# Thought's weights prepared inside the first attention, its first chain ahead of the next scans' preparation, and its gate behind the rounds

## The chip, the cores and the metric

The kernel runs on one core of one Trainium2 chip. The metric is the device time of one execution, in microseconds, the median of three runs. Five engines share the core: TensorE (PE in the profile; its weight loads are a row of their own, PEld), VectorE (DVE), ScalarE (ACT), GpSimd (POOL) and SyncE (SP), which issues the DMAs. Each engine works through its own instructions in program order and waits on semaphores for the others.

## The reference

The whole is a small decoder of four layers with four batches of 256 tokens, 256 channels, all in float32. Each part is added to x and followed by a plain layer norm. The parts that matter here, cut down:

```python
# part 0: attention of 16 heads of 128, one shared key and value head, rotary, causal
x = layernorm(x + attn0(x))
# part 1: a selective scan over another input, ctx, gated by x
def ssm(ctx, x):
    u = silu(conv4(ctx @ in_proj.T) + conv_b)           # 256 channels, 256 steps
    dt, Bm, Cm = split(u @ x_proj.T, [8, 16, 16])
    delta = softplus(dt @ dt_proj.T + dt_b)
    state = exp(delta * A) * state + delta * u * Bm      # 16 states per channel
    y = sum_n(state * Cm) + D * u
    return y * silu(x)
x = layernorm(x + ssm(ctx, x))
# part 2: the "thought": one vector per batch, from the last token
t = (ln(x[:, -1]) * in_g + in_b) @ agg_w + agg_b
for _ in range(4):
    h = gelu((ln(t) * pn_g + pn_b) @ d1_w + d1_b)        # 256 -> 1024
    t = t + h @ d2_w + d2_b                              # 1024 -> 256
out = x + sigmoid(x @ gate_w + gate_b) * (t @ bc_w + bc_b)
x = layernorm(x + ln(out) * out_g + out_b)
# part 3: attention with 16 heads of 16, 4 key and value heads
x = layernorm(x + attn3(x))
# part 4: a second selective scan over ctx with other weights, gated by x
x = layernorm(x + ssm(ctx, x))
# parts 5 to 11: experts, a state space layer, cross attention, a ternary
# feed-forward, linear attention, attention to ctx, a float8 feed-forward
```

The scans of parts 1 and 4 depend on ctx alone until their last product with silu(x). They can therefore run long before x is known, and the kernel uses that.

## The kernel before, in words

x stays in SBUF as eight tiles of 128 tokens by 256 channels, and its transpose xT beside it. The parts follow each other; when one runs, the weights of the next are loaded by a call named `more`. Work is issued from Python in one order; the order of instructions on each engine follows that, with moves that the scheduler makes from what each instruction waits for.

**First attention and first scans.** `run_mqa` has 32 steps (4 batches, 4 groups of 4 heads, 2 tiles of queries). A step n divides its softmax (`shares`), makes the scores of n+1 and the queries of n+4, puts two steps of the first scans (called l0x) beside that, then turns its probabilities on TensorE, and multiplies them with the values (`sums`); the `output` matmul follows a step later. At n = 6 it calls `more`, which loads the thought's weights. For each batch whose attention and scans are done, `gate_pair` (L534) multiplies y with silu(x), transposes it and adds it to x. This runs two steps into the next batch, and for the last batch after the loop; then L388 starts the preparation of the second scans (l1x).

**Scans.** `_steps` of class `Scans` is a generator. Its first part is the preparation: four taps by DMA and GpSimd, eight convolution matmuls of 512 columns into one PSUM bank, Silu on the whole (L126), two matmuls for dt, B and C (L474 and a DMA to DRAM), and softplus as Abs, Exp, Ln on du of 128x2048 and a `scalar_tensor_tensor` on VectorE (L120). GpSimd then makes du = delta * u (L123). After it come 64 steps (4 batches, 16 states): a DMA that spreads B and C over the partitions, two Exp for dA on ScalarE, s = du * B on VectorE (L111), the scan instruction (L520), s * C on VectorE, and a sum on TensorE one or two steps later. In all a step takes VectorE three instructions.

**Thought.** `run_thought` first prepares its weights: the columns of d2 are centred, so that the mean of t's increment is zero, by a reduction over 128x2048 on VectorE (L129) and eight Identity on ScalarE; constants `over`, `less`, `power`, `pick` and `centre` are filled by GpSimd and VectorE; d1b is joined with pn_b @ d1 by `quarters` (four quarters of the 1024 columns on four groups of 32 partitions); d1 is scaled with pn_g; cb is the centred d2b. Then it makes the gate of all eight tiles, 16 matmuls, 8 additions, one Sigmoid. After these comes the chain: the last tokens are transposed (L684), normed, multiplied with agg, centred. The four rounds follow, each: square, variance by matmul, a power on GpSimd, scaling, `quarters` with d1, Gelu, two transposes (L728), a copy (L730), `quarters` with d2, a copy (L734), sums with `pick`. GpSimd meanwhile makes gx = gate * bc_b + x and xb = x + out_b. Then 24 scan steps of l1x are issued, `K.scans.beside(24)`. The tail is per batch: `gated` multiplies the gate with t @ bc_w and adds gx on GpSimd, `moments` takes its statistics with a root on GpSimd (L169 and a power at L123), `added` norms it into x, and `settle` applies the part's layer norm (L160, L161, L117) and transposes x.

**Second attention.** `run_gqa` starts with memsets of kn, qn and vt on GpSimd (L994 to L1001), projects and norms its queries and keys, and runs with one scan step of l1x beside each of its own steps.

TensorE's accumulators live in PSUM[...]. The thought has a pool `thp` of three, `thf` of one; the scans have one.

## Time and profile before

| | us |
|---|---|
| three runs | 2458.55, 2461.45, 2464.18 |
| median | 2461.45 |
| profiled execution, its own time | 2461.66 |
| its span, first to last instruction | 2459.9 |
| TensorE busy in the span | 2267.6 (92%) |
| VectorE busy | 1464.3 (60%) |
| ScalarE busy | 801.9 (33%) |
| GpSimd busy | 288.5 (12%) |
| mean granted TensorE clock | 0.947 |

The page gives busy time for the whole span. The change touches about its first third, and there the shares are different from stage to stage, so the views that are read are the table of stretches (busy time of each engine between two times) and the instructions of one engine in order of time. In the latter, a line is start, length, engine, line of the code, operation, output<-inputs, shape, count, and in square brackets the idle time of the engine just before and the instruction that ended it. "x4" means that four like instructions are gathered in the line and the length is the sum of them. A clock of 0.50 means that TensorE was granted half of its full speed. Times are from the span's start. Marks: the first scan of l0x starts at 87.95, the first attention ends at about 366, the first scan of l1x starts at 439.23, the thought's tail begins at 499.60, the second attention's first matmul starts at 527.71.

### The profile page before, as it was taken

What the parts mean: (1) busy time and instruction counts of PE and PEld (TensorE: products, weight loads), DVE (VectorE), ACT (ScalarE), POOL (GpSimd) and SP (SyncE); (2) the same over time, 40 slices, a digit from 0 to 9 for tenths busy, and PEclk for the clock granted to TensorE, in tenths of its full rate; (3) what the DMA queues carried; (4) which work ended last, traced back from release to release, by engine and by line L of the source; (5) the groups of instructions that cost most, each with busy time, mean ns of one, the idle gap of its engine ahead of it and who ended that gap; (6) DMA issues with size and microseconds to landing.
All of it is one profiled execution on the core that took longest, in us unless ns stands there. A gap on an engine that the chain in (4) does not pass through costs nothing. (4 is left out here: it accounts for less than half of the span.)

```text
span 2459.9 us, 28697 instructions
## 1 busy us (share of the span) xinstructions
PE 2267.6 (92%) x10620; PEld 1520.1 (62%) x10624; DVE 1464.3 (60%) x2986; ACT 801.9 (33%) x1781; POOL 288.5 (12%) x455
## 2 busy tenths in 40 slices
PE   8899997769996999899999999999999988899997
PEld 4566763335433555536888888888776543476774
DVE  4799982888985211280455544445556677774566
ACT  3577664513441111162211111111022244343434
POOL 0000014130010322200011000110210002100001
PEclk9999997767887999999999999999998899999999
DMA  6222221312213544220222112110100002100000
GB/s 201 61 60 60 53 61 27 80 41 48 52 39 101 164 131 127 81 78 9 73 82 87 46 46 73 47 63 31 46 22 1 20 18 71 41 1 1 1 1 18
DMA packets 132835, 138.99 MB, mean 57 GB/s; under 512 B 13876, under 2 KB 120726, under 8 KB 130904
## 3 DMA queue, kind: packets, MB, share of 16 engines
q1 hardware_dynamic: 132696, 137.16, 19.5%
q8 instruction: 84, 1.38, 0.2%
q14 instruction: 55, 0.45, 0.1%
HBM read 134.27 MB, written 2.85 MB: 56 GB/s over the span
## 5 line engine op out<-in xcount | busy, mean ns | idle before, releaser
L132 PE MATMUL ps<-xw,xcT 128*128 128x256 f32 (+1 forms) x2304 | 518.9, 382 | 0.3 <-ACT YT L126 0.3
L132 PEld LDWEIGHTS ps<-xw,xcT 128*128 128x128 f32 x2304 | 430.8, 190 | 64.0 <-issue 1.9
L132 PE MATMUL sc<-kT,qT 32*128 32x256 f32 (+2 forms) x1024 | 239.2, 404 | 9.6 <-DVE qn L129 9.2
L132 PEld LDWEIGHTS sc<-kT,qT 128*128 128x128 f32 (+1 forms) x1024 | 152.6, 200 | 86.0 <-issue 52.4
L111 DVE TENSOR_TENSOR xp<-ps,xb 128x256 f32<-128x256 f32 x96 | 40.4, 421 | 230.7 <-PE ps L132 230.6
L126 ACT ACTIVATE dA<-delta,negA 128x255 f32<-128x255 f32 x256 | 118.2, 501 | 142.0 <-DVE s L520 139.1
L132 PE MATMUL ssmps<-s,idz 128*128 128x512 f32 x256 | 146.7, 678 | 18.9 <-DVE s L111 18.0
L520 DVE TENSOR_TENSOR_SCAN s<-dA,s 128x512 f32<-128x512 f32 x128 | 155.0, 1218 | 2.6
L126 ACT ACTIVATE p<-sc,nm 128x256 f32<-128x256 f32 (+1 forms) x256 | 112.0, 444 | 96.5 <-DVE nm L129 90.5
L111 DVE TENSOR_TENSOR hT<-u,a 128x512 f32<-128x512 f32 x48 | 33.1, 690 | 184.0 <-PE u L132 184.0
L126 ACT ACTIVATE sq<-xp 128x1024 f32<-128x1024 f32 x24 | 25.4, 1057 | 314.1 <-DVE xp L111 314.1
L132 PE MATMUL o<-pT,vt 128*128 128x256 f32 (+1 forms) x352 | 116.2, 452 | 12.3 <-ACT pT L332 11.9
L169 POOL TENSOR_SCALAR rstd<-mv 128x2 f32<-128x2 f32 x48 | 11.8, 245 | 887.5 <-DVE mv L161 877.7
L129 DVE TENSOR_REDUCE qn<-sc 128x2 f32<-128x480 f32 (+1 forms) x192 | 87.0, 505 | 37.9 <-PE sc L132 36.4
L126 ACT ACTIVATE e<-sT 128x512 f32<-128x512 f32 x128 | 70.9, 591 | 108.4 <-PE sT L132 108.2
L132 PE MATMUL sT<-q,kT 32*128 32x256 f32 (+1 forms) x384 | 102.3, 508 | 3.5 <-ACT e L126 3.3
L1474 DVE TENSOR_TENSOR_SCAN dec<-xT,idz 128x256 f32<-128x256 f32 (+1 forms) x192 | 89.7, 535 | 21.5 <-DMA xT<-ad 21.5
L129 DVE TENSOR_REDUCE nm<-sc 128x2 f32<-128x512 f32 (+1 forms) x128 | 77.3, 612 | 41.2 <-PE sc L132 40.7
L126 ACT ACTIVATE a<-g 128x512 f32<-128x512 f32 x48 | 28.7, 598 | 206.2 <-PE g L132 203.4
L111 DVE TENSOR_TENSOR s<-du,bc 128x512 f32<-128x512 f32 x128 | 87.7, 691 | 11.0 <-POOL du L123 7.7
L123 POOL TENSOR_TENSOR xp<-xp,rn 128x128 f32<-128x128 f32 x96 | 35.2, 403 | 476.9 <-DVE rn L1406 476.9
L132 PE MATMUL g<-xT,wj 128*128 128x512 f32 x192 | 90.3, 593 | 0.7 <-ACT rows L100 0.7
(503 smaller groups left out, 4027.2 us busy)
## 6 DMA issues: line engine op xcount, KB each, us to landing
bc<-bcd SPq DMA_DIRECT2D x128, 256.0 KB, 4.6
xw<-in_l2a_xw_dram SPq DMA_DIRECT2D x24, 768.0 KB, 4.8
xT<-ad SPq DMA_DIRECT2D x12, 1024.0 KB, 4.3
wj<-in_l1f_gate_dram SPq DMA_DIRECT2D x48, 128.0 KB, 2.7
wj<-in_l1f_up_dram SPq DMA_DIRECT2D x48, 128.0 KB, 2.9
wj<-in_l1f_down_dram SPq DMA_DIRECT2D x48, 128.0 KB, 3.1
sel<-cwd SPq DMA_DIRECT2D x32, 192.0 KB, 3.2
sel<-cwd SPq DMA_DIRECT2D x32, 128.0 KB, 3.5
```

Source lines behind the costliest of these rows:

```text
L111: self.nc.vector.tensor_tensor(out=out, in0=a, in1=b, op=op)
L123: self.nc.gpsimd.tensor_tensor(out=out, in0=a, in1=b, op=op)
L126: self.nc.scalar.activation(out, in_, func, **kw)
L129: self.nc.vector.tensor_reduce(out=out, in_=in_, axis=AX.X, op=op, **kw)
L132: self.nc.tensor.matmul(out, lhsT=lhsT, rhs=rhs, start=start, stop=stop)
L169: self.nc.gpsimd.tensor_scalar(out=out, in0=in_, scalar1=add, scalar2=None, op0=ADD)
L520: nc.vector.tensor_tensor_scan(out=s.rearrange("p c l -> p (c l)"), data0=dA.rearrange("p c l -> p (c l)"), data1=s.rearrange("p c l -> p ...
L1474: nc.vector.tensor_tensor_scan(out=dec[:, k, h, :], data0=ap[:, h, at(bb, k, j) : at(bb, k, 2)], data1=K.idz[:, 0 : (2 - j) * P], initial=0.0,
```

## The change

(a) The thought's weights are prepared by a generator `ready_thought`, which `run_mqa` creates at n = 6 and advances by one piece per step from n = 10 on. Two things in it are new: the sums of d2 are made on ScalarE by eight Copy instructions with an accumulated output in place of the reduction on VectorE, and its two PSUM tiles come from the shared pool of transposes. The tiles that it fills live in the weights' pool.

(b) The preparation of the l1x scans is no longer started at the end of the first attention but in `run_thought`, after the first chain (`th`, `ct` and the first part of `last`) and ahead of the rounds.

(c) In the preparation of both scans Exp and Ln are issued per half of du (128x1024), and du = delta * u is a VectorE instruction.

(d) The gate's matmuls and additions come behind the rounds, three tiles in each of the first two and two in the third, with a PSUM pool of one bank for them; the Sigmoid is issued in the third round.

(e) gx and xb are gone: bc_b is added into the PSUM tile by one more matmul with the identity, gate + x is a VectorE instruction, and out_b is added to x in place on GpSimd in the tail.

(f) Five memsets of the second attention go from GpSimd to VectorE.

```diff
--- before.py
+++ after.py
@@ -374,7 +374,9 @@
             if n in (2, 3, 4, 5):
                 rest.pop(0)()
             if n == 6:
-                more()
+                ready = ready_thought(K, more()) if K.fused(0) else iter(())
+            if n > 9:
+                next(ready, None)
             K.scans.beside(2)
             turn(n)
             if n:
@@ -385,7 +387,6 @@
         output(N - 1)
         if K.fused(0):
             gate_pair(K, wk, y, B - 1)
-            K.scans.begin("l1x")
 
 
@@ -480,11 +481,12 @@
                 K.ts(delta[:, c, s], ps, cols[:, c, 1:2], None, ADD)
                 K.act(du[:, c, s], ps, AF.Abs, bias=cols[:, c, 1:2])
-        K.act(du, du, AF.Exp, scale=-1.0)
-        K.act(du, du, AF.Ln, bias=K.eps[1.0])
+        for func, kw in ((AF.Exp, dict(scale=-1.0)), (AF.Ln, dict(bias=K.eps[1.0]))):
+            for c in range(DC):
+                K.act(du[:, c, :], du[:, c, :], func, **kw)
         for c in range(DC):
             K.stt(delta[:, c, :], delta[:, c, :], 0.0, du[:, c, :], MAX, ADD)
-            K.ptt(du[:, c, :], delta[:, c, :], u[:, c, :], MUL)
+            K.tt(du[:, c, :], delta[:, c, :], u[:, c, :], MUL)
         turn = 0
         self.y = u
@@ -557,8 +559,6 @@
             ctx.enter_context(K.turns())
             for b in range(B):
                 gate_pair(K, wk, y, b)
-        if pre == "l0x":
-            K.scans.begin("l1x")
     return run
 
@@ -579,7 +579,67 @@
     w["cols"] = K.load(wp, "l0f_cols", [P, 2, DC])
     w["pn"] = K.load(wp, "l0f_pn", [P, 2, DC])
     w["rows"] = K.load_rows(wp, "l0f_rows")
+    for n, cols in (("mean", 8), ("junk", D), ("over", P), ("less", P), ("centre", P), ("power", B), ("pick", B), ("cb", DC)):
+        w[n] = wp.tile([P, cols], F32, name=n)
     return w
+
+def quarters(K, ps, lhsT, rhs, n, start):
+    for c in range(DC):
+        for g in range(4):
+            K.mm(ps[32 * g : 32 * g + n], lhsT(c, g), rhs(c, g), start and c == 0, c == DC - 1)
+
+def quarter(d1):
+    return lambda c, g: d1[:, c, g * D : (g + 1) * D]
+
+def ready_thought(K, w):
+    nc, d1, d2, mean = K.nc, w["d1"], w["d2"], w["mean"]
+
+    for f in range(8):
+        K.act(w["junk"], d2[:, f, 0:D], AF.Copy, scale=1.0 / D, accum_out=mean[:, f : f + 1])
+        if f % 4 == 3:
+            yield
+    K.ts(d2[:, :, D], mean, 1.0, None, MUL)
+    K.ts(mean, mean, -1.0, None, MUL)
+    yield
+    for f in range(8):
+        K.act(d2[:, f, 0:D], d2[:, f, 0:D], AF.Identity, bias=mean[:, f : f + 1])
+        if f % 2:
+            yield
+    nc.gpsimd.memset(w["over"], 1.0 / D)
+    nc.gpsimd.memset(w["less"], -1.0 / D)
+    K.ts(w["centre"], K.ident, 1.0 / D, None, SUB)
+    nc.gpsimd.memset(w["power"], -0.5)
+    pick = w["pick"]
+    K.ptt(pick, K.ident[:, 0:B], K.ident[:, 32 : 32 + B], ADD)
+    for g in (2, 3):
+        K.ptt(pick, pick, K.ident[:, 32 * g : 32 * g + B], ADD)
+    yield
+    ps = K.tp.tile([P, 512], F32, name="ps", tag="tp")[:, 0:D]
+    K.mm(ps, K.ident, w["d1b"], True, False)
+    quarters(K, ps, lambda c, g: w["pn"][:, 1, c : c + 1].to_broadcast([P, B]), quarter(d1), B, False)
+    nc.scalar.copy(w["d1b"], ps)
+    yield
+    for c in range(DC):
+        K.act(d1[:, c, :], d1[:, c, :], AF.Copy, scale=w["pn"][:, 0, c : c + 1])
+        yield
+    ps = K.tp.tile([P, 512], F32, name="ps", tag="tp")
+    centred(K, w, ps[:, 0:DC].unsqueeze(2), w["cols"][:, 1, :].unsqueeze(2))
+    nc.vector.tensor_copy(w["cb"], ps[:, 0:DC])
+    yield
+
+def centred(K, w, ps, src):
+    for c in range(DC):
+        for k in range(DC):
+            K.mm(ps[:, c, :], w["centre" if c == k else "less"], src[:, k, :], c + k == 0, c + k == 2)
 
 def run_thought(K, w, more):
@@ -592,6 +652,7 @@
         wk = ctx.enter_context(tc.tile_pool(name="th2", bufs=2))
         ctx.enter_context(K.turns())
         pm = ctx.enter_context(tc.tile_pool(name="thp", bufs=3, space=PSUM))
+        gp = ctx.enter_context(tc.tile_pool(name="thg", bufs=1, space=PSUM))
         spare = ctx.enter_context(tc.tile_pool(name="thf", bufs=1, space=PSUM))
         def moments(t, rows, n):
@@ -621,63 +682,12 @@
             K.ts(r, t[:, 0, :], mv[:, 0, 0:1], rstd, SUB, MUL)
             return r
-
-        d1, d2 = w["d1"], w["d2"]
-        mean = one.tile([P, 8], F32, name="mean")
-        K.reduce(mean, d2[:, :, 0:D], ADD)
-        K.ts(d2[:, :, D], mean, 1.0 / D, None, MUL)
-        K.ts(mean, mean, -1.0 / D, None, MUL)
-        for f in range(8):
-            K.act(d2[:, f, 0:D], d2[:, f, 0:D], AF.Identity, bias=mean[:, f : f + 1])
...
+        if K.first == 2:
+            for _ in ready_thought(K, w):
+                pass
+        d1, d2, d1b = w["d1"], w["d2"], w["d1b"]
         d2b = w["cols"][:, 1, :]
-        cb = one.tile([P, DC], F32, name="cb")
-        nc.vector.tensor_copy(cb, centred(d2b.unsqueeze(2), 1)[:, :, 0])
-
-        gate = one.tile([P, NT, D], F32, name="gate")
-        for i in range(NT):
-            ps = pm.tile([P, D], F32, name="ps", tag="mm")
-            for c in range(DC):
-                K.mm(ps, K.xT[:, c, i * P : (i + 1) * P], w["gate"][:, c, :], c == 0, c == DC - 1)
-            K.tt(gate[:, i, :], ps, row["gate_b"], ADD)
-        K.act(gate, gate, AF.Sigmoid)
+        over, power, pick, cb = w["over"], w["power"], w["pick"], w["cb"]
         last = K.tp.tile([B, D], F32, name="last", tag="tp")
         for c in range(DC):
@@ -694,17 +704,17 @@
                 K.mm(ps[:, c, :], w["agg"][:, k, c * P : (c + 1) * P], xn[:, k, :], c + k == 0, c + k == 2)
         th = one.tile([P, DC, B], F32, name="th")
         K.tt(th, ps, wide(w["cols"][:, 0, :], B), ADD)
-        ct = centred(th, B)
+        ct = pm.tile([P, DC, B], F32, name="ps", tag="mm")
+        centred(K, w, ct, th)
         K.stt(th, wide(d2b, B), 4.0, th, MUL, ADD)
         last = spare.tile([P, B], F32, name="last")
         for k in range(DC):
             K.mm(last, over, th[:, k, :], k == 0, False)
-        gx = one.tile([P, NT, D], F32, name="gx")
-        xb = one.tile([P, NT, D], F32, name="xb")
-        if K.first == 2:
-            K.scans.begin("l1x")
+        K.scans.begin("l1x")
+        gate = one.tile([P, NT, D], F32, name="gate")
+        gates = iter(range(NT))
         for k in range(4):
             sq = wk.tile([P, DC, B], F32, name="sq")
             K.act(sq, ct, AF.Square)
@@ -720,7 +730,7 @@
             K.tt(cs, ct, wide(cb, B), ADD)
             ps = pm.tile([P, D], F32, name="ps", tag="mm")
             K.mm(ps, K.ident, d1b, True, False)
...
             ct = pm.tile([P, DC, B], F32, name="ps", tag="mm")
@@ -737,24 +747,29 @@
             for c in range(DC):
                 K.mm(ct[:, c, :], add[:, c * P : (c + 1) * P], pick, False, c == DC - 1)
             K.mm(last, add[:, D : D + 1].to_broadcast([P, P]), pick, False, k == 3)
+            for i in itertools.islice(gates, 3):
+                ps = gp.tile([P, D], F32, name="gps")
+                for c in range(DC):
+                    K.mm(ps, K.xT[:, c, i * P : (i + 1) * P], w["gate"][:, c, :], c == 0, c == DC - 1)
+                K.tt(gate[:, i, :], ps, row["gate_b"], ADD)
+            if k == 2:
+                K.act(gate, gate, AF.Sigmoid)
         mean = wk.tile([P, B], F32, name="lastmean")
         nc.vector.tensor_copy(mean, last)
         thT = wk.tile([P, DC, B], F32, name="thT")
         K.tt(thT, ct, again(mean, DC), ADD)
-        for i in range(NT):
-            K.ptt(gx[:, i, :], gate[:, i, :], row["bc_b"], MUL)
-            K.ptt(gx[:, i, :], gx[:, i, :], K.x[:, i, :], ADD)
-            K.ptt(xb[:, i, :], K.x[:, i, :], row["out_b"], ADD)
         K.scans.beside(24)
         def gated(b):
             ps = pm.tile([P, D], F32, name="ps", tag="mm")
+            K.mm(ps, K.ident, row["bc_b"], True, False)
             for c in range(DC):
-                K.mm(ps, thT[:, c, b : b + 1].to_broadcast([P, P]), w["bc"][:, c, :], c == 0, c == DC - 1)
+                K.mm(ps, thT[:, c, b : b + 1].to_broadcast([P, P]), w["bc"][:, c, :], False, c == DC - 1)
             for i in (2 * b, 2 * b + 1):
                 K.tt(gate[:, i, :], gate[:, i, :], ps, MUL)
-                K.ptt(gate[:, i, :], gate[:, i, :], gx[:, i, :], ADD)
+                K.tt(gate[:, i, :], gate[:, i, :], K.x[:, i, :], ADD)
+                K.ptt(K.x[:, i, :], K.x[:, i, :], row["out_b"], ADD)
             return moments(gate[:, 2 * b : 2 * b + 2, :], P, 2)
         def added(b, mv, rstd):
@@ -762,7 +777,7 @@
                 i = 2 * b + t
                 g = gate[:, i, :]
                 K.stt(g, g, mv[:, t, 0:1], row["out_g"], SUB, MUL)
-                K.stt(K.x[:, i, :], g, rstd[:, t : t + 1], xb[:, i, :], MUL, ADD)
+                K.stt(K.x[:, i, :], g, rstd[:, t : t + 1], K.x[:, i, :], MUL, ADD)
                 K.settle(i)
         ahead = gated(0)
@@ -991,11 +1006,11 @@
         kn = one.tile([P, NT, 4, 32], F32, name="kn")
         vt = one.tile([P, NT, 4, 2, 32], F32, name="vt")
         ones = one.tile([P, 2, 32], F32, name="ones")
-        nc.gpsimd.memset(kn[:, :, :, 16:32], 0.0)
-        nc.gpsimd.memset(kn[:, :, :, 16:17], 1.0)
-        nc.gpsimd.memset(qn[:, :, :, 16:32], 0.0)
-        nc.gpsimd.memset(vt[:, :, :, 0, 16:32], 0.0)
-        nc.gpsimd.memset(vt[:, :, :, 1, 0:16], 0.0)
+        nc.vector.memset(kn[:, :, :, 16:32], 0.0)
+        nc.vector.memset(kn[:, :, :, 16:17], 1.0)
+        nc.vector.memset(qn[:, :, :, 16:32], 0.0)
+        nc.vector.memset(vt[:, :, :, 0, 16:32], 0.0)
+        nc.vector.memset(vt[:, :, :, 1, 0:16], 0.0)
         nc.gpsimd.memset(ones, 0.0)
         for j in range(2):
             nc.gpsimd.memset(ones[:, j, 16 * j : 16 * j + 16], 1.0)
```

## The prediction

> **What bounds the kernel now.** The change touches the piece from the first attention to the second one, so I read the table of stretches over it before anything else. After the stretch come us, then busy us (and instructions) of each engine, the granted TensorE clock, DMA share and GB/s.
>
> ```profile
> core 0: us, PE busy (x) PEld busy (x) DVE busy (x) ACT busy (x) POOL busy (x), PEclk, DMA share, GB/s
> 87.00:365.00 278.00, 256.76 (x1092) 176.62 (x1091) 260.00 (x429) 185.32 (x529) 13.13 (x19) 0.98 0.26 59
> 365.00:439.00 74.00, 55.06 (x199) 27.68 (x197) 21.41 (x50) 32.38 (x44) 32.19 (x49) 0.75 0.11 30
> 439.00:500.00 61.00, 47.74 (x196) 19.46 (x196) 57.10 (x84) 31.56 (x64) 2.90 (x3) 0.81 0.46 95
> 500.00:528.00 28.00, 7.66 (x24) 4.11 (x24) 23.36 (x70) 2.13 (x6) 14.68 (x24) 0.62 0.09 20
> 528.00:765.00 237.00, 216.39 (x1156) 105.42 (x1155) 191.44 (x321) 84.50 (x170) 26.46 (x55) 0.82 0.23 52
> ```
>
> In the first attention (87 to 365) VectorE is busy 94% and TensorE 92%: two full engines, ScalarE at 67%. In 439 to 500 VectorE alone is full, 57 of 61: the 24 scan steps that are forced ahead of the thought's tail. Between them, 365 to 439, nothing is full: VectorE has 21 of 74 us of work. Those 74 us are waiting, and what bounds them is a chain from the last attention output to the first scan of layer 1. So I followed that chain by time on VectorE, GpSimd and ScalarE (start, length, what, and the idle time ahead with its releaser):
>
> ```profile
> 374.76 0.17 DVE L161 BATCH_NORM_AGGREGATE mv<-stats 128x2 f32<-128x6 f32 x1
> 374.84 2.25 DVE L129 TENSOR_REDUCE mean<-w_d 128x8 f32<-128x2048 f32 x1
> 377.01 0.17 DVE L161 BATCH_NORM_AGGREGATE mv<-stats 128x2 f32<-128x6 f32 x1
> ...
> 382.41 1.00 DVE L117 TENSOR_SCALAR x<-x,mv,rstd 128x256 f32<-128x256 f32 x2 [4.28 <-POOL rstd L123]
> ```
> ```profile
> 375.97 2.81 POOL L123 TENSOR_TENSOR xb<-x,r_l0f_rows 128x256 f32<-128x256 f32 x4
> 379.19 1.79 POOL L996 MEMSET qn<- 128x2048 f32 x1
> 380.97 0.21 POOL L169 TENSOR_SCALAR rstd<-mv 128x2 f32<-128x2 f32 x1
> ```
> ```profile
> 424.40 1.28 ACT L126 ACT_TABLE_LOAD   x1
> 425.69 1.91 ACT L126 ACTIVATE du<-du 128x2048 f32<-128x2048 f32 x1
> 427.51 0.36 ACT L734 COPY add<-ps 128x257 f32<-128x257 f32 x1
> 427.88 1.28 ACT L126 ACT_TABLE_LOAD   x1
> 429.18 2.00 ACT L126 ACTIVATE du<-du,eps 128x2048 f32<-128x2048 f32 x1
> ```
> ```profile
> 431.21 2.36 DVE L120 SCALAR_TENSOR_TENSOR delta<-delta,du 128x1024 f32<-128x1024 f32 x2 [9.45 <-ACT du L126]
> 432.52 5.55 POOL L123 TENSOR_TENSOR du<-delta,u 128x1024 f32<-128x1024 f32 x2 [12.07 <-DVE delta L120]
> 438.10 0.69 DVE L111 TENSOR_TENSOR s<-du,bc 128x512 f32<-128x512 f32 x1 [4.46 <-POOL du L123]
> 439.23 1.22 DVE L520 TENSOR_TENSOR_SCAN s<-dA,s 128x512 f32<-128x512 f32 x1
> ```
>
> The reader is to see three things. The last layer norm's root waits on GpSimd behind xb and memsets while a 2.25 us reduction of a weight sits between the two aggregates: x is normalized at 382.41 instead of some 4 us after 374.10, when the statistics start. Then TensorE does weights' work and 16 gate matmuls, so that the thought's first transposes come at 404.17 (L684) and its first square at 411.07. Last, du goes through Exp and Ln in whole 128x2048 pieces and its product through GpSimd for 5.55 us, before the first scan at 439.23. The rounds run under this: the four start at 411.07, 431, 450.17 and 463.20, so two of 20 and 19 us and then two of 13 and 15.7.
>
> **The change, step by step.**
>
> *Into the first attention* go eight sums of d2 on ScalarE. Nearest rows: its Exp with an accumulator of 256 columns, 0.47 us, at a pitch of 0.45: 8 × 0.45 = 3.6. Eight Identity at the present 0.41: 3.3. Two d1 scalings at 1.15: 2.3. One copy: 0.36. The functions force two switches of table beyond those there. A switch takes 1.28 in the third fence above; 2.6. In all 12.2 us on an engine with 93 us idle in 278. **A rule against it:** the Trainium skill, "ScalarE: Activation LUTs", section "What ACT_TABLE_LOAD costs", puts a switch at about 2.7 us with the drain ahead of it; two would be 5.3, and the du halves below, where six loads lie on the path, would cost 8 us more than I count. The row disagrees: the copy hT ends at 424.38, the load starts at 424.40 and du's Exp at 425.69, so no drain is seen. I take the row and keep the page's 2.7 for the slow end. TensorE gets 3.0 us (the d1b matmul 0.6, the quarters 1.3, nine small centred ones 1.1). VectorE gets the l0x scans' two du products, 128x1024 each, 2 × 1.3 from twice the 0.69 row, and 0.7 of small operations: 3.2. The d2 load is issued at 27.26 and landed by 39, so the first sums at about 43 don't wait. Against it, the l0x scans start sooner: their du product on GpSimd (5.55 in the same code) becomes 2.6 on VectorE, pipelined by halves, so 87.95 becomes about 85.7. What hides the ScalarE work is its 33% idle time; but queued behind it, in order, are one step's softmax and the shares of the next, for which TensorE's transposes wait, and the exponentials of the scans. If all of it is hidden: −2.2 and some 1 of TensorE. If TensorE's and VectorE's 3.0 + 3.2 are paid in full: +6. I take **+2**, range −1 to +6, since both queues are 92 to 94% full and take some of what is added.
>
> *The join.* The reduction goes; the xb adds and memsets leave GpSimd's queue ahead of the root. From the statistics at 374.10: two aggregates and the root's two steps (0.5 each) let x's normalization start at about 376 and give xT at about 378.6 rather than 385.76: −7.1. The thought's chain is now first: its transposes at 378.8 rather than 404.17, the square 7 us later as now (404.17 to 411.07, less 0.5 to 1 us of clock): about 387, 24 us sooner. Round 0 no longer shares TensorE with the preparation at half clock: 12 us, close to round 2's 13; it ends at about 399, and round 1's Gelu, the last thing ahead of the tables of the scans, at 406.5.
>
> *The preparation of l1x* is started after the chain, so that its convolutions (5.3 us at half clock, 3.7 at full), taps' DMAs and dt matmuls fall inside round 0. What sets its end is ScalarE's queue, in program order from about 406.5: six table loads (Exp, Ln, Exp, Ln, the gate's Sigmoid, Exp) 7.7; du halves 2 × 0.96 and 2.0 for Ln; one Abs 0.69; hT and add 0.73; the Sigmoid 1.91 (row of 128x2048 at 406.52); a square 0.16; first dA pair 1.0: 16.1, so the first scan at about 422.5. If the Sigmoid falls behind dA it is 418.4. I take 421 against 439.23: 18.2 sooner. VectorE's du products (1.3 each) lie under the other half's Ln; by then three s products of the scans are done too, 1.8. So the lead is 20 where the 24 scan steps begin. Those keep VectorE full at 2.32 each, so the lead is carried, unless rounds 2 and 3, now with 3 + 2 gate tiles in them on TensorE, end last: they took 28.7 us with 3.8 of waiting on VectorE, and the steps last 56. I charge 1: **−19**, from −14 (Sigmoid and drains on the path: five drains of 1.4 would take 7, some under the rounds) to −22.6 (scan at 418.4).
>
> *The tail*, 500 to 528. gx and xb go from GpSimd. VectorE gets eight adds of 128x256, 0.31 to 0.41 each: 2.5 to 3.3; it is busy 23.4 of 28, so 4.6 us are free. The additional ident matmul is four times 0.6 on a TensorE busy 7.7 of 28. GpSimd's out_b adds (0.7 each by the xb row) lie ahead of the roots in its queue. All hidden: 0, as the old gate adds on GpSimd held VectorE too; all paid: +4. **+2**.
>
> *The second attention.* Its memsets go from GpSimd to VectorE, ahead of the first scans or between them: 2 us of gaps to hide in before 421; 0. It starts at another phase of TensorE's clock (granted 0.82 over 528 to 765): ±4, only in the range. Everything after 765 is the same code.
>
> **The sum:** the profiled execution's own time is 2461.66, the span 2459.9 and 1.8 around it; that is 0.2 above the median of the runs, 2461.45, so nothing is to be corrected. 2461.66 + 2 − 19 + 2 = 2446.7, less 0.2: **2446**, 0.6% faster. Own range: all good ends together, −1 − 22.6 + 0, give 2438; two of the three bad ends at a time (+6 − 14 + 2, +2 − 14 + 4, +6 − 19 + 4) lie between −6 and −9, so 2454.
>
> **Rivals.**
>
> *Half the gain, 2457.* TensorE's granted clock is 0.50 around 416 to 440. For: with preparation and gate taken out of 383 to 404, TensorE is emptier still, and the rounds are small matmuls; then rounds 0 and 1 stay near 16 each, Gelu of round 1 comes at 415, the scan at 431: −8 instead of −18, +2 +2. Against: round 2 took 13 us at no high clock.
>
> *All added work shows, 2461.* ScalarE's 12.2, TensorE's 3.0 and VectorE's 3.2 less the 2.2 fill the first attention: 16 of the 19 are given back there, and 2 in the tail. Speaks for it that softmax and dA stand in one queue; against, ScalarE's 93 us of idle time.
>
> *Slower, 2468.* One mechanism: at the two table switches near steps 10 to 20 the softmax of one step comes behind weights' work, the transposes behind it miss their turn on TensorE, and the forced two scan steps each wait for dA: the pipeline falls one whole step of (366 − 28)/32 = 10.5 us behind, with ScalarE's 12.2 not under it: +22.7 in place of +2. It decides once the first attention ends later than about 383, where the 19 less the tail's 2 is used up. Against: scores are made a step ahead and VectorE's idle 18 us are spread.
>
> **Chances.** Forecast 0.68; half the gain 0.15; all shows 0.08; slower 0.09. What a measurement of this kernel can tell from no change is about 0.2%, 4.9 us. Of the half-gain case some lies near the edge; with the third case that gives same 0.10, slower 0.10, faster 0.80. The range leaves out 0.1 above and 0.1 below or less: 2436 (scan at 418.4, tail free, and 2 of clock) to 2458, the half-gain case within.
>
> **What would show it.** No reduction between the aggregates, and the normalization not waiting for GpSimd's root; transposes of the last tokens at about 379; du's first Exp at about 408 and the first l1x scan at about 421; the tail from about 480 and the second attention's first matmul near 510; the end of the first attention at 366 to 370. Wrong if that end is past 375, or if the scan starts after 430 with the rounds still 16 or more.

## The result and the profile after

The changed kernel took 2455.44 us in the median of 12 runs (2449.13 to 2459.20), the kernel before 2462.52 in 12 runs beside them; the ratio is 0.9963 with a 95% interval of 0.9951 to 0.9975, so 0.37% faster, 6 to 12 us. The forecast was 2446 and its range 2436 to 2458: the sign and the range hold, the gain is smaller than forecast. The profiled execution took 2449.13, the fastest of the 12; its span is 2447.4. The execution of before that was profiled took 2461.66, near its median, so the two profiles differ by more than the medians do.

The table of stretches of the changed kernel, cut where its own stages change: from the attention's last output addition to the first l1x scan, to the tail, to the second attention, to the last layer norm behind the second scans' gate, and the rest. Columns as in the prediction.

```profile
core 0: us, PE busy (x) PEld busy (x) DVE busy (x) ACT busy (x) POOL busy (x), PEclk, DMA share, GB/s
365.35:423.87 58.52, 46.35 (x215) 23.74 (x214) 24.91 (x58) 29.98 (x40) 6.22 (x12) 0.91 0.14 38
423.87:484.13 60.26, 46.35 (x155) 18.23 (x156) 54.77 (x77) 28.50 (x60) 3.12 (x2) 0.78 0.41 96
484.13:514.46 30.33, 9.56 (x26) 4.86 (x25) 26.27 (x80) 2.13 (x5) 14.57 (x24) 0.56 0.09 21
514.46:747.72 233.26, 211.42 (x1156) 101.96 (x1156) 190.40 (x319) 84.68 (x170) 26.56 (x55) 0.86 0.22 51
747.72:2447.35 1699.63, 1614.68 (x7698) 1144.57 (x7698) 874.32 (x1975) 422.95 (x874) 188.42 (x281) 0.97 0.17 52
```

And the kernel before, cut at the same five events:

```profile
366.33:439.23 72.90, 53.73 (x194) 26.70 (x192) 21.22 (x52) 32.38 (x44) 32.24 (x49) 0.74 0.12 30
439.23:499.60 60.37, 47.34 (x195) 19.46 (x196) 56.55 (x83) 31.28 (x63) 2.85 (x2) 0.81 0.46 95
499.60:527.71 28.11, 7.77 (x25) 3.82 (x23) 23.47 (x72) 2.13 (x5) 14.68 (x24) 0.62 0.10 22
527.71:764.03 236.32, 216.68 (x1156) 105.71 (x1156) 190.76 (x319) 84.79 (x170) 26.46 (x55) 0.82 0.23 51
764.03:2459.88 1695.85, 1610.89 (x7694) 1142.24 (x7698) 874.09 (x1975) 422.90 (x874) 188.56 (x281) 0.98 0.17 52
```

Most of the gain is in the first row: 72.9 became 58.5, and GpSimd's 32 us in it became 6. The second row did not move, the tail became 2.2 longer, the second attention 3.1 shorter, and the first attention ended 1.0 sooner. Up to 764.03 the changed kernel is 16.3 ahead. In the last row, where both run the same instructions, 3.8 of it is gone again.

At the join, VectorE and then GpSimd of the changed kernel, in order of time:

```profile
373.78 0.17 DVE L161 BATCH_NORM_AGGREGATE mv<-stats 128x2 f32<-128x6 f32 x1
374.00 0.48 DVE L1009 MEMSET kn<- 128x512 f32 x1
374.40 0.12 DVE L161 BATCH_NORM_AGGREGATE mv<-stats 128x2 f32<-128x6 f32 x1
...
375.66 0.73 DVE L117 TENSOR_SCALAR x<-x,mv,rstd 128x256 f32<-128x256 f32 x2 [0.57 <-POOL rstd L123]
```
```profile
374.62 0.22 POOL L169 TENSOR_SCALAR rstd<-mv 128x2 f32<-128x2 f32 x1 [1.57 <-DVE mv L161]
374.92 0.71 POOL L123 TENSOR_TENSOR rstd<-rstd,power 128x2 f32<-128x2 f32 x1
```

No reduction lies between the aggregates, and GpSimd's root starts 0.22 after the second of them starts. VectorE waits 0.57 for it, where it waited 4.28. ScalarE's queue up to the first dA:

```profile
406.45 0.38 ACT L126 ACTIVATE h<-ps 128x256 f32<-128x256 f32 x1
406.84 1.28 ACT L126 ACT_TABLE_LOAD   x1
408.14 1.06 ACT L126 ACTIVATE du<-du 128x1024 f32<-128x1024 f32 x1
...
416.17 1.15 ACT L126 ACTIVATE du<-du,eps 128x1024 f32<-128x1024 f32 x1
417.34 1.28 ACT L126 ACT_TABLE_LOAD   x1
418.63 1.91 ACT L126 ACTIVATE gate<-gate 128x2048 f32<-128x2048 f32 x1
420.45 0.36 ACT L744 COPY add<-ps 128x257 f32<-128x257 f32 x1
420.83 1.28 ACT L126 ACT_TABLE_LOAD   x1
422.12 0.51 ACT L126 ACTIVATE dA<-delta,negA 128x255 f32<-128x255 f32 x1
```

The table loads follow each other and their work without a gap (du's Ln ends at 417.32, the next load starts at 417.34), so the trace's 1.28 for a switch was the right price here, and not the 2.7 with a drain of the Trainium skill ("ScalarE: Activation LUTs", "What ACT_TABLE_LOAD costs"). The Sigmoid lies ahead of the first dA. VectorE at the same place:

```profile
418.61 1.23 DVE L111 TENSOR_TENSOR du<-delta,u 128x1024 f32<-128x1024 f32 x1
419.87 2.50 DVE L111 TENSOR_TENSOR s<-du,bc 128x512 f32<-128x512 f32 x4
423.80 0.16 DVE L115 TENSOR_SCALAR rstd<-ps 128x4 f32<-128x4 f32 x1 [1.43 <-PE ps L132]
423.87 1.23 DVE L522 TENSOR_TENSOR_SCAN s<-dA,s 128x512 f32<-128x512 f32 x1
```

The s products are ready at 422.4 and the two Exp that make the first step's dA at 423.1, but the first scan stands behind a small instruction of the third round (`rstd`, one over the standard deviation), for which VectorE waits 1.43. Of this wait the scan itself loses the last 0.8, from 423.09 to 423.87.

### The profile page after: what moved, and what is told of

It reads as the page before. It is cut to its first block, busy times and chain, and to the rows that moved or that the text cites. A ratio compares the mean times of both kernels' runs of the same rounds, so it can differ in the third digit from the quotient of the medians.

```text
span 2447.4 us, 28725 instructions
## 1 busy us (share of the span) xinstructions
PE 2259.7 (92%) x10632; PEld 1516.4 (62%) x10632; DVE 1472.1 (60%) x3002; ACT 808.9 (33%) x1803; POOL 257.9 (11%) x422
## 5 line engine op out<-in xcount | busy, mean ns | idle before, releaser
L132 PE MATMUL sc<-kT,qT 32*128 32x256 f32 (+2 forms) x1024 | 240.4, 402 | 10.6 <-DVE qn L129 10.3
L126 ACT ACTIVATE dA<-delta,negA 128x255 f32<-128x255 f32 x256 | 119.0, 501 | 144.3 <-DVE s L522 142.7
L132 PE MATMUL u<-xT,wj 128*128 128x512 f32 x192 | 90.4, 592 | 0.0
```

Source lines behind the costliest of these rows:

```text
L126: self.nc.scalar.activation(out, in_, func, **kw)
L132: self.nc.tensor.matmul(out, lhsT=lhsT, rhs=rhs, start=start, stop=stop)
```

## The experiments

Whole times of this kernel scatter by some 20 us from run to run, so the times below are told with their intervals. Each ratio is against executions of the kernel before on the same chip. Stages are compared as distances from one event: the start of the second of the two last additions with which the attention's output goes into x. "First square" is ScalarE's Square that opens the rounds, "last norm" the layer norm behind the second scans' gate, "the piece" all up to it, and "the rest" what follows to the end. Each variant has one profile, the kernel before three, the changed kernel two; so a difference of a few us in the table is one execution's.

| us from that addition | first square | first l1x scan | tail | last norm | rest after it |
|---|---|---|---|---|---|
| before | 44.7, 44.0, 46.6 | 72.9, 72.2, 74.0 | 133.3, 131.7, 132.9 | 397.7, 392.7, 395.8 | 1695.9, 1699.4, 1706.6 |
| changed | 20.9, 20.9 | 58.5, 59.9 | 118.8, 118.9 | 382.4, 382.9 | 1699.6, 1704.8 |
| without (a) | 23.9 | 65.1 | 122.0 | 387.7 | 1709.4 |
| without (b) | 20.9 | 58.9 | 117.9 | 383.5 | 1699.6 |
| without (c) | 20.9 | 60.9 | 119.0 | 382.5 | 1710.8 |
| without (d) | 23.8 | 89.3 | 146.6 | 412.1 | 1706.3 |
| without (e) | 25.2 | 62.8 | 130.4 | 393.7 | 1716.5 |
| without (f) | 21.7 | 59.4 | 118.3 | 384.0 | 1701.4 |
| Sigmoid behind the steps | 20.9 | 60.0 | 118.6 | 383.6 | 1706.3 |
| (a), (d), (e) alone | 21.7 | 60.1 | 120.2 | 385.8 | 1700.0 |
| tail's additions on GpSimd | 20.9 | 58.5 | 118.7 | 381.2 | 1704.9 |

**The changed kernel again.** No edit.

> The changed kernel once more. In its profile the last layer norm ahead of the experts (the end of the second scans' gate) stood at 747.72 us against 764.03 before, 16.3 sooner, but the end only 12.5 sooner: the piece from 748 on took 1699.7 us instead of 1695.9, with 3.5 of it lost at one place around 1808 to 1825, where TensorE's granted clock fell to 0.55. Theory 1 (the gain of the piece is steady, and what is missing from the medians is lost later to the granted clock, differently from run to run): that norm comes at 746 to 750 again, the rest takes 1695 to 1702, and the clock at the place of 1808 differs. Theory 2 (the piece itself scatters, most of all in the second attention): the norm moves by 4 us or more and the rest stays within 1 of 1699.7. Median 2452 to 2458 by both.

Median 2458.41 of 12 runs against 2463.40 of before, ratio 0.9976 (0.9953 to 0.9998). The norm came at 750.51, 2.8 later than in the first profile, 2.3 of it already there at the attention's last addition; counted from that addition the piece repeats within 0.5, though the first scan within it is 1.4 later. The rest took 1704.8. Both numbers lie just outside what theory 1 had named (746 to 750, 1695 to 1702), but it holds in kind: the rest moved by 5.2, the piece by less.

**The kernel before again, twice.** No edit.

> The kernel before once more, for its stages. In its first profile the last norm of the second scans' gate stood at 764.03 us, 397.7 after the attention's last addition, and the rest took 1695.9; in nine profiles of the changed kernel and its variants the same rest took 1699.6 to 1716.5. Theory 1 (the rest is a draw of TensorE's granted clock between about 1808 and 2010, and the first profile of before drew well): the norm at 762 to 766, 397 to 399 after the addition, and the rest 1699 to 1712. Rival 1 (the change lengthens the rest): the rest 1695 to 1697 again. Rival 2 (the first profile of before was late in the piece): the norm at 755 to 760.

> As for the other repeat of the kernel before: norm at 762 to 766 and the rest 1699 to 1712 by theory 1; the rest 1695 to 1697 by rival 1; the norm at 755 to 760 by rival 2. The two repeats differ in the rest by more than 2 us where the draw decides, by less than 1 where the code does.

2462.11 and 2469.81. The norm stood at 760.9 and 761.4, between theory 1 and rival 2: counted from the addition, the first profile had been 1.9 to 5.0 later in the piece, most of it in its second attention (236.3 against 232.9 and 234.7). The rest took 1699.4 and 1706.6, so rival 1 falls: the 1695.9 of the first profile was the shortest of all fourteen. Where the rest is made, three profiles show best: before, the changed kernel and the variant without (e), each from the same place in the stage of the cross attention to the same place in the linear attention, cut by hand to within a us or two, in this order.

```profile
1817.00:1984.00 167.00, 156.72 (x1063) 98.14 (x1062) 100.55 (x239) 43.87 (x77) 6.96 (x14) 0.90 0.05 16
```
```profile
1800.00:1970.00 170.00, 159.07 (x1057) 100.16 (x1055) 100.56 (x239) 43.87 (x77) 6.95 (x14) 0.88 0.05 16
```
```profile
1812.00:1995.00 183.00, 173.71 (x1065) 106.27 (x1065) 100.77 (x239) 43.97 (x77) 6.96 (x14) 0.80 0.05 15
```

VectorE and ScalarE do the same work in the same time; TensorE is granted 0.90, 0.88 and 0.80 of its clock, and the stretch is 167, 170 and 183 us long. Over the fourteen profiles the time at half clock in the rest goes from 81 us (rest 1695.9) through 88 to 89 (1699.4 to 1700.0, four of them), 97 (1701.4), 104 (1704.8 and 1704.9), 105 to 112 (1706.3 to 1709.4, four) and 117 (1710.8) to 129 (1716.5). The same idle time can be followed by different clocks. TensorE in the profile of before, then in that of the changed kernel, at the same matmul:

```profile
1824.98 1.10 PE L132 MATMUL sc<-kT,qT 32*128 32x256 f32 x4 [1.29 <-DVE qn L129]
```
```profile
1808.27 1.39 PE L132 MATMUL sc<-kT,qT 32*128 32x256 f32 x4 [1.29 <-DVE qn L129]
```

Behind it the clock of before stays full for 6.9 us more and is then half for 3.4; that of the changed kernel is half from 1808.9 on, for 13.7.

**Weights where they were, part (a) undone.** The tiles and the room of the two removed tiles stand in the thought's pool again, so that the preparation comes at the join and not earlier.

```diff
-                ready = ready_thought(K, more()) if K.fused(0) else iter(())
-            if n > 9:
-                next(ready, None)
+                more()
...
-    for f in range(8):
-        K.act(w["junk"], d2[:, f, 0:D], AF.Copy, scale=1.0 / D, accum_out=mean[:, f : f + 1])
+    K.reduce(mean, d2[:, :, 0:D], ADD)
...
-        if K.first == 2:
-            for _ in ready_thought(K, w):
-                pass
+        for n, cols in (("mean", 8), ("over", P), ("less", P), ("centre", P), ("power", B), ("pick", B), ("cb", DC)):
+            w[n] = one.tile([P, cols], F32, name=n)
+        pad = one.tile([P, 2 * NT, D], F32, name="pad")
+        nc.gpsimd.memset(pad[:, 0, 0:1], 0.0)
+        for _ in ready_thought(K, w):
+            pass
```

> Only part (a) undone: the thought's weights are prepared where they were, at the join, by the reduction on VectorE, and nothing of it runs in the first attention. Theory 1 (12 us of ScalarE's added work are mostly hidden in the first attention, and the join gets shorter): the first attention's last addition comes 1 to 3 us sooner than the changed kernel's 372.45, the first square of the rounds at 391 to 394 instead of 386.2, the first l1x scan 3 to 5 later than 423.87; the time 2 to 4 above the changed kernel. Rival (the added work costs in the attention what it saves at the join): the last addition 4 or more sooner, and the time equal to the changed kernel's within 1.

2460.40, ratio 0.9972 (0.9948 to 0.9995). The last addition of the gate stood at 372.65, beside 372.45 and 374.71 with (a): the added 12 us of ScalarE cost nothing in the attention that these profiles can tell. Without (a) the first square is 3.0 later, the first scan 5 to 6.6, the tail 3.1. Theory 1 holds in direction, with the square less late and the scan later than it had named. The time is 2.0 above the changed kernel's on the same chip, which the scatter hides; that the attention would end 1 to 3 sooner is not seen. The rival falls with that.

**The preparation started early, part (b) undone.**

```diff
             gate_pair(K, wk, y, B - 1)
+            K.scans.begin("l1x")
...
-        K.scans.begin("l1x")
```

> Only part (b) undone: the preparation of the l1x scans is started at the end of the first attention again, ahead of the thought's chain. Theory 1 (what sets the first scan is ScalarE's queue of tables, which is issued in the same place either way): the chain's first square 2 to 4 later than 386.2, the first l1x scan within 3 of 423.87, the time within 3 of the changed kernel. Rival (as the prediction had it, the order chain first is what brings the scan forward): the first scan at 430 or later, the time 6 or more above.

2455.06, ratio 0.9965 (0.9943 to 0.9987). First scan 58.9, tail 117.9, and the first square, which theory 1 had 2 to 4 later, is where it was: part (b) by itself brings nothing, and the rival, which was the prediction's own account, falls. With nothing in its way the preparation is taken up early in either order. In the changed kernel, where it is issued behind the chain, TensorE has convolution matmuls before the copies into xT, which start at 374.44:

```profile
364.81 2.74 PE L132 MATMUL ssmps<-ctxp,tap 128*128 128x512 f32 x6
```

**Whole du, part (c) undone in both scans.**

```diff
-        for func, kw in ((AF.Exp, dict(scale=-1.0)), (AF.Ln, dict(bias=K.eps[1.0]))):
-            for c in range(DC):
-                K.act(du[:, c, :], du[:, c, :], func, **kw)
+        K.act(du, du, AF.Exp, scale=-1.0)
+        K.act(du, du, AF.Ln, bias=K.eps[1.0])
...
-            K.tt(du[:, c, :], delta[:, c, :], u[:, c, :], MUL)
+            K.ptt(du[:, c, :], delta[:, c, :], u[:, c, :], MUL)
```

> Only part (c) undone in both scans: Exp and Ln on the whole du, and the product on GpSimd. Theory 1: the tail of the preparation is Exp 1.9, table 1.3, Ln 2.0, two sums on VectorE 2.4 and 5.6 on GpSimd, with two table loads fewer; the first l1x scan 4 to 6 later than 423.87; the first l0x scan at 88 instead of 83.8 with the end of the first attention not moved by more than 1.5; the time 4 to 6 above the changed kernel. Rival (the two more table loads of the halves cost what the product on VectorE saves): the first l1x scan within 1.5 of 423.87 and the time within 1.5.

2459.64, ratio 0.9968 (0.9942 to 0.9993). The first scan is 1 to 2.4 later, and the 24 steps then take 58.1 rather than 59.0 and 60.3, so that the tail begins at 119.0, no later than with (c). That is nearer to the rival: the halves bring the scan forward by a little, and the steps wait that much more. The first l0x scan came at 88.13, as named, against 83.81 and 85.69 with (c); whether that moves the attention's end isn't told apart from scatter.

**The gate ahead of the chain, part (d) undone.**

```diff
+        gate = one.tile([P, NT, D], F32, name="gate")
+        for i in range(NT):
+            ps = pm.tile([P, D], F32, name="ps", tag="mm")
+            for c in range(DC):
+                K.mm(ps, K.xT[:, c, i * P : (i + 1) * P], w["gate"][:, c, :], c == 0, c == DC - 1)
+            K.tt(gate[:, i, :], ps, row["gate_b"], ADD)
+        K.act(gate, gate, AF.Sigmoid)
         last = K.tp.tile([B, D], F32, name="last", tag="tp")
...
-            for i in itertools.islice(gates, 3):
...
-            if k == 2:
-                K.act(gate, gate, AF.Sigmoid)
```

> Only part (d) undone: the gate's 16 matmuls, 8 additions and Sigmoid are issued ahead of the thought's chain again. Distances are counted from the start of the first attention's last addition of its output, and the changed kernel's own two profiles agree on them within 0.1 for the first square (20.9), within 1.4 for the first l1x scan (58.5 and 59.9) and within 0.5 for the last norm of the second scans' gate (382.4 and 382.9). Theory (most of the 24 us by which the chain came sooner is the gate's place): first square at 28 to 34; first l1x scan at 58 to 63, since the Sigmoid's table load and 1.9 us leave the queue ahead of the first dA while the rounds come later; last norm at 383 to 387. Rival (the scheduler puts the gate behind the chain anyway, where its operands wait for xT): the first square within 1.5 of 20.9 and all else within 1.5.

2477.53, ratio 1.0051 (1.0030 to 1.0071): slower than before. The first square moved by 2.9 only, less than expected, but the first scan by 29 to 31, which nothing had foreseen. TensorE and then ScalarE of this variant:

```profile
379.12 3.62 PE L132 MATMUL ps<-w_l0f_gate,xT 128*128 128x256 f32 x16
...
386.51 0.37 PE L673 MATMUL ps<-idz,r 4*128 4x4 f32 x2 [2.69 <-DVE r L111]
...
391.39 1.02 PE L132 MATMUL last<-th,over 128*128 128x4 f32 x4 [0.26 <-DVE th L120]
392.26 5.84 PE L132 MATMUL ssmps<-ctxp,tap 128*128 128x512 f32 x8
```
```profile
383.23 1.91 ACT L126 ACTIVATE gate<-gate 128x2048 f32<-128x2048 f32 x1 [2.03 <-DVE gate L111]
385.05 0.67 ACT L126 ACTIVATE u<-ssmps,w_l1x_cols 128x512 f32<-128x512 f32 x1
391.17 0.18 ACT L126 ACTIVATE sq<-ps 128x8 f32<-128x8 f32 x1 [5.45 <-PE ps L132]
398.13 0.69 ACT L126 ACTIVATE u<-ssmps,w_l1x_cols 128x512 f32<-128x512 f32 x1 [6.79 <-PE ssmps L132]
...
407.95 1.91 ACT L126 ACTIVATE u<-u 128x2048 f32<-128x2048 f32 x1
```

The square is hardly late because half of the gate's matmuls run from 364.1 to 369.6 already, ahead of the last tiles of x, and the other half, the first line above, takes 3.6 us. In the kernel before all of them lay behind the weights' work, with parts of the preparation between, from 386.99 to 404.3. The copy of u that frees the scans' one PSUM bank (385.05) stands behind the Sigmoid. (A bank is the tile of 128x512 that a convolution accumulates in; the scans have one. The trace has two entries for each matmul of the code, 32 for the convolutions, eight for each of four fillings of the bank.) The next convolutions, issued behind the chain since (b), stand behind the chain's matmuls, which wait for VectorE: 16 of the 32 entries are still left at 392.26, and the first eight of them take 5.84 at a clock of 0.63, where the last eight take 3.70 at full clock. Silu on u comes at 407.95, where the changed kernel has it at 386.31. As this trace reads, part (b) does harm with the gate in front, while with the gate behind it does nothing; no run has the gate in front and the preparation early with the other parts in place. The profiled execution was the slowest of the six. Its last norm is 29.5 later than the changed kernel's, while the two ratios of the changed kernel put the loss in whole times at 18 to 22.

**gx and xb, part (e) undone.**

```diff
+        for i in range(NT):
+            K.ptt(gx[:, i, :], gate[:, i, :], row["bc_b"], MUL)
+            K.ptt(gx[:, i, :], gx[:, i, :], K.x[:, i, :], ADD)
+            K.ptt(xb[:, i, :], K.x[:, i, :], row["out_b"], ADD)
         K.scans.beside(24)
...
-            K.mm(ps, K.ident, row["bc_b"], True, False)
...
-                K.tt(gate[:, i, :], gate[:, i, :], K.x[:, i, :], ADD)
-                K.ptt(K.x[:, i, :], K.x[:, i, :], row["out_b"], ADD)
+                K.ptt(gate[:, i, :], gate[:, i, :], gx[:, i, :], ADD)
```

> Only part (e) undone: gx and xb on GpSimd again, no matmul for bc_b, no addition of x on VectorE, and out_b added ahead of time. The tail from its first product to the second attention's first projection is 30.3 us in all profiles with part (e) and 28.1 before. Theory (the eight additions on VectorE cost the 2 us that were charged): the tail is 28 to 28.5, and, as the xb additions come into GpSimd's queue at the join again, the root there waits and the first square comes 1 to 4 later than 20.9; the last norm 0 to 3 sooner or later than 382.6. Rival (the tail is longer by GpSimd's additions of out_b ahead of the roots or by the extra matmuls' banks, and the join is shorter because the xb additions are gone): the tail 28 to 28.5 likewise but the first square 5 or more later.

2464.89, ratio 1.0005 (0.9984 to 1.0027): without (e) the gain is gone. The tail is 28.1 as expected, 2.2 shorter, and the first square 4.3 later, between theory and rival. But the 24 steps take 67.6 instead of 59 to 60, which neither had. GpSimd and VectorE of this variant:

```profile
424.98 2.26 POOL L123 TENSOR_TENSOR gx<-gate,r_l0f_rows 128x256 f32<-128x256 f32 x2 [16.32 <-ACT gate L126]
...
434.02 1.40 POOL L123 TENSOR_TENSOR gx<-gx,x 128x256 f32<-128x256 f32 x2
435.38 1.02 POOL L123 TENSOR_TENSOR rstd<-rstd,power 128x4 f32<-128x4 f32 x1
436.37 1.86 POOL L123 TENSOR_TENSOR gx<-gate,r_l0f_rows 128x256 f32<-128x256 f32 x2
438.19 3.23 POOL L123 TENSOR_TENSOR gx<-gx,x 128x256 f32<-128x256 f32 x2
```
```profile
428.24 1.23 DVE L522 TENSOR_TENSOR_SCAN s<-dA,s 128x512 f32<-128x512 f32 x1
436.43 0.17 DVE L111 TENSOR_TENSOR tT<-ps,rstd 128x8 f32<-128x8 f32 x1 [6.97 <-POOL rstd L123]
...
437.56 3.34 DVE L522 TENSOR_TENSOR_SCAN s<-dA,s 128x512 f32<-128x512 f32 x2
```

gx waits for the Sigmoid, which is late now, so it falls among the rounds: the third round's root on GpSimd stands behind twelve instructions of gx, and VectorE waits 6.97 for it with the scans queued behind. Part (e) had been priced by the join and the tail; most of its worth is here. This profile too is of the slowest of its executions; the last norm is 11.1 later than the changed kernel's, and the ratios put the loss in whole times at 7 to 10.

**The memsets, part (f) undone.**

```diff
-        nc.vector.memset(kn[:, :, :, 16:32], 0.0)
...
+        nc.gpsimd.memset(kn[:, :, :, 16:32], 0.0)
...
```

> Only part (f) undone: five memsets on GpSimd. Theory (they stood in front of the root at the join before, and on VectorE they lie in its gaps): normalization of the last tiles 11 to 15 us after the attention's last addition instead of 10.3, last norm 1 to 4 later than 382.6. Rival (without the xb additions ahead of them GpSimd has room for them): normalization within 0.5 of 10.3 and the first square 0.3 to 1 sooner than 20.9, as the copy of the last tokens waited for a memset of 1.76 us on VectorE; last norm within 1.

2454.91, ratio 0.9967 (0.9948 to 0.9986). Normalization at 11.0 instead of 10.3, the tail at 118.3 instead of 118.8. The join and the last norm (1.1 to 1.6 later) are at the low edge of the theory, the tail is not later at all; the part is worth less than these profiles can tell.

**The Sigmoid behind the steps.**

```diff
-            if k == 2:
-                K.act(gate, gate, AF.Sigmoid)
...
         K.scans.beside(24)
+        K.act(gate, gate, AF.Sigmoid)
```

> A new arrangement on top of the changed kernel: the gate's Sigmoid is issued behind the 24 scan steps, so that on ScalarE it comes after the first six pairs of dA, just ahead of the third round's Gelu, instead of ahead of the first dA. Theory (ScalarE's queue sets the first scan): one table load and the Sigmoid, 3.2 us, leave the path; first l1x scan at 55 to 57 after the attention's last addition instead of 58.5 to 59.9, tail 2 to 3 sooner than 118.8, last norm 379.5 to 381. Rival (the 24 steps wait for something else, a Gelu with two table loads between the dA): the scan 3 sooner and the tail within 1 of 118.8.

2456.11, ratio 0.9971 (0.9945 to 0.9997). The first dA moved from 422.12 to 418.78 as planned, and the scan did not: 60.0. VectorE of this variant:

```profile
417.50 1.22 DVE L120 SCALAR_TENSOR_TENSOR delta<-delta,du 128x1024 f32<-128x1024 f32 x1 [2.60 <-ACT du L126]
421.94 0.16 DVE L115 TENSOR_SCALAR rstd<-ps 128x4 f32<-128x4 f32 x1 [3.21 <-PE ps L132]
422.02 1.22 DVE L111 TENSOR_TENSOR du<-delta,u 128x1024 f32<-128x1024 f32 x1
```

The third round's rstd now stands ahead of the second half's du product, and VectorE waits 3.21 for its matmul: a wait of the same size has taken the place of the one removed. Both theories had the scan 3 sooner, and both missed it; the tail within 1 of 118.8 is the rival's, but not for its reason.

**Parts (a), (d) and (e) alone.** The edits without (b), (c) and (f) together.

> The kernel before with parts (a), (d) and (e) alone: weights in the first attention, gate behind the rounds, no gx and xb; (b), (c) and (f) left as they were. Undone singly, these three moved the last norm (382.4 to 382.9 after the attention's last addition) by 0 to 1.5 at most. Theory (they bring nothing, together neither): the norm at 381 to 385, the tail's start 117.5 to 120 after the addition, the time 0.995 to 0.998 of before. Rival (one covers for the other: with the preparation begun early and du whole on GpSimd, the first scan comes later than each alone showed): the first l1x scan at 63 or later instead of 58.5 to 61, the norm at 386 or later.

2459.64, ratio 0.9996 (0.9979 to 1.0013). In its profile the first scan is at 60.1, the tail at 120.2 and the last norm at 385.8, the last two just past the theory's ranges and all short of the rival's. By its profile this kernel has three quarters of the piece's gain (9.6 of 12.8 at the last norm, the mean of the three profiles of before being 395.4), the other three parts together up to 3. Its time isn't told apart from before's, where the theory had 0.995 to 0.998: the interval has room for a gain of 5 us, not of 9.6. So the piece's gain doesn't reach the end whole in this variant either, and why stays open.

**The tail's additions on GpSimd.**

```diff
-                K.tt(gate[:, i, :], gate[:, i, :], K.x[:, i, :], ADD)
+                K.ptt(gate[:, i, :], gate[:, i, :], K.x[:, i, :], ADD)
```

> One edit on the changed kernel: the eight additions of x to the gate in the tail go to GpSimd, in front of its additions of out_b. The tail takes 30.3 us in all profiles with the additions on VectorE, 28.1 with gx. Theory (VectorE's eight additions, some 3 us, are what lengthens the tail): 27.5 to 29. Rival (the latency of the chain is what counts, and a GpSimd addition of 0.72 us in it with another 0.72 queued ahead of the roots is dearer than 0.42 on VectorE): 31 to 35. Nothing ahead of the tail moves by more than 1.

2457.13, ratio 0.9990 (0.9970 to 1.0010). The tail takes 33.5: the rival. On GpSimd an addition takes 0.72 to 1.04 and stands in front of the roots; in the tail VectorE's 0.42 is the cheaper place, though the tail is 2.2 longer with it than with gx made beforehand. At the last norm, however, nothing of the 3.2 is left (381.2 against 382.4 and 382.9), since the second attention of this profile took 229.0 and not 233. What a longer tail costs in the end is therefore not shown by it.

None of the variants is told apart from the changed kernel as faster.

## Why the prediction was right, and where it was off

The work moved into the first attention was hidden and the join became shorter as forecast; the lead carried through the steps was put too high, and the cause (b) was not one.

*The first attention, +2.* It was hidden, as the trace's 33% of idle ScalarE let expect, and the 2 were too much: the last output addition starts at 366.3, 368.2 and 365.6 before, at 365.4 and 367.6 after. The rivals "all added work shows" and "slower" fall with it; the second needed an end past 383.

*The join, −7.1, and the chain.* x is normalized at 375.66 for a forecast of 376, the last tokens are transposed at 377.70 for 378.8, the first square stands at 386.24 for 387, round 0 ends at 399.80 for 399, round 1's Gelu at 406.45 for 406.5, du's Exp at 408.14 for 408. Counted from the last addition, xT is complete 7.2 sooner (12.3 after it, where it was 19.4) and x is normalized 5.8 sooner. "Half the gain", with rounds near 16 and the scan at 431, falls by its mechanism, though the measured 2455.44 lies nearer to its 2457 than to 2446. The chain's 24 us are a joint effect: without (a), (d) or (e) alone the first square is 3.0, 2.9 and 4.3 later, and (a), (d) and (e) together bring it from 44 to 47 down to 21.7.

*Up to the steps, −19: this is the term that was mis-sized.* It measured 13.8 (the first scan 59.2 after the addition in the mean of two profiles, 73.0 in the mean of three before). The queue of ScalarE had been worked out at 422.5, and 421 was taken because the Sigmoid might fall behind the first dA. It did not, and when it was made to, the scan stayed, held by a round's rstd on VectorE. In the first profile the scan came at 423.87: 1.5 for the Sigmoid, 0.6 for a queue that ended at 423.1 and 0.8 for the rstd, 2.9 against 421. With the addition 1.0 sooner in that profile, and the second profile's scan 1.4 later still, the scan's 18.2 measured 13.8. (The 418.4 for a Sigmoid behind dA was itself 1 too early: without one load and the Sigmoid, 3.2, the sum gives 419.3.) The products made ahead, priced at 1.8, were made (four of them, 2.5 us of work), but the 24 steps take as long as before, 59.0 and 60.3 against 59.0 to 60.4, so nothing is left of the 0.8 that the forecast kept of them. In the profiles of before and after VectorE's waits in the steps are 4.1 and 6.9: for the rounds' matmuls and roots and, new in the latter, for a transfer of B and C. So the tail began at 484.13 and the second attention at 514.46, where 480 and 510 had been named.

*The account of who brings it* was wrong in part. The order chain before preparation, part (b), was counted among the causes; undone it changes nothing. The preparation was also mis-sized: the 5.3 us of convolutions that were to fall inside round 0 are eight entries of the trace of before, which has 32, and 24 of them had run by 379 already; in the changed kernel all 32 are over by 384.1, before round 0. What carries the gain is the gate behind the rounds, which is worth 28 us at the tail in one profile with the other parts in place, gx off GpSimd, worth 11.5 likewise, and the early weights, 3 at the tail and 5 at the last norm. The first two depend on one another, since a late Sigmoid makes a late gx, and the 28, as that trace reads, holds the harm that (b) does when the gate is in front. Edits that were priced one by one, each against the old kernel's queues, do not add up to the whole.

*The tail, +2*: 30.3 against 28.1, +2.2. *The second attention, 0*: 233.3 and 233.6 against 232.9 to 236.3.

*Everything after 765, "the same code".* The same code took 1695.9 to 1716.5. The sum was made against the profile of before that drew the shortest of all; at the last norm the profiles before average 762.1 and the changed kernel's two 749.1, a gain of 13.0 for a forecast of 15, and the medians show 7.1 and 5.0. That the piece came so near is luck in part: the steps brought 5.2 less, the tail 0.2 less, but the first attention cost 2.2 less than charged and the second was 1.2 shorter, which no step of the forecast had named. In the rest the profiles of before average 1700.6 (three), the two of the changed kernel 1702.2, its nine variants 1706.1. Whether the earlier arrival makes the rest longer on the average, which the medians would need, or this is chance, stays open: no run here gives TensorE's clock in the rest another draw by design.

## What to carry to other kernels

Find where a moved instruction will stand in every queue, and what waits in front of it there: on VectorE a round's 0.16 us instruction held up the work behind it for 0.8 to 7 us. Undo parts singly after a success, because the part that was believed to matter may be idle, and two others may hold each other up. Where whole times scatter by more than the gain, compare stages from an event inside the program.

## What was not expected of the hardware

TensorE's granted clock falls in steps of 3.4 us, to half, at different places in executions of one program. Over the fourteen profiles the length of the rest, 1695.9 to 1716.5, rises with the time at half clock, 81 to 129 us. Between the shortest and the longest, 16 of the 20.6 us lie in the stages around 1800 to 2000 us, where TensorE stops for a us or so between matmuls. The Trainium skill says so much of the window ("TensorE: Matmul & The Clock Gate", "Part 1: The HAM clock gate (the "warmup" mystery)": a window of 3.4 us that runs freely and doesn't start with the kernel). That this window is why the clock falls at other places each time is not shown by any run here. The page puts the penalty of ramping up from the slow clock below 1% of a typical kernel; the spread here, which is of falls in the middle, is 0.8% of the span, and is yet more than the gain that was to be measured.

In the variant without (e), scans on VectorE that take 1.22 us took 1.68 and 1.75 while GpSimd made gx, whose additions took 1.64 instead of 0.72. The skill's lock on the port pair that both engines use ("SBUF — State Buffer", "SBUF: two separate sides": one of the two blocks for the whole of the other's instruction) fits those numbers, but no run separates it from another cause; the prediction hadn't priced it.
